# First attention layer: value projections of units 2 and 3 moved into turns 1 and 2, and those turns put into the fixed order

## The chip, the cores and the metric

One core of one Trainium2 chip runs the whole kernel. The metric is the device time of one execution in microseconds (us). Names used below: PE is the matrix engine (TensorE), DVE the vector engine, ACT the scalar engine, POOL the GpSimd engine, SP the engine that here only issues DMAs. PEld is the loading of weights into PE.

## The reference

A batch of two images, 512 channels of 64 x 64 pixels in float32, passes four residual layers. The change lies in the first, a local attention with 8 heads of 64 channels, of which this is the core:

```python
q = l2norm(gn(x) @ W_q + b_q);  q_scaled = (q + query_embedding) * softplus(temperature)
k, v = gn(x) @ W_kv + b_kv;     k = l2norm(k)             # per head
local = q_scaled . k over the 3 x 3 neighbours            # 9 scores per pixel and head
pool  = q_scaled . l2norm(k_pool)                         # 256 pooled tokens
a = softmax([local, pool])
lt = q . learnable_tokens + bias + a[:9]
out = sum over 9 neighbours lt * v + a[9:] @ v_pool
x = x + out @ W_proj + b_proj
```

The pooled tokens come from a projection with GELU, a mean over 4 x 4 pixels and a layer norm. The other three layers (deformable attention, a mixture of max pools, a linear attention) are not touched.

## The kernel before

**Layout.** Channels lie on the 128 partitions, in four chunks (cc, 0 to 3), two heads to a chunk. A unit is 1024 pixels (16 image rows) of one chunk: UN = 4 units to a chunk, 16 units in all, numbered 0 to 15. The class `Local` computes the layer, once for each of the two images. The images of keys (`kx`) and values (`vx`) of one chunk are kept with a border of zeros, so that the nine neighbours are nine shifted views.

**Turns.** `run` (L2020) goes through turns i = -4 to 16. In turn i different units are at different stages, and each stage is a Python generator that issues the instructions of one step and yields; `in_turn` takes one step of each stage after the other, ten steps to a turn. The stages of turn i:

- `norms` (L2359): for the keys and queries projected in the turn before, sums of squares on PE (L2369), a transpose on DVE (L2372), some thirteen small DVE instructions for the inverse roots (L2375 to L2382), a transpose back (L2384).
- `tap_products` and `tap_sums` for unit i+1: the query times nine shifted key images on DVE (L2447), summed over a head's channels on PE (L2474, four column tiles of 32), exponential on ACT (L2482).
- `attend` for unit i: scores against the pooled keys (L2499), exponentials on ACT (L2503), pooled values (L2509), the halves of the sums on POOL (L2518), sums of the softmax on PE (L2525, L2528), reciprocal on DVE (L2553 to L2561); then the weights go to rows in DRAM (L2566) and come back spread over the 64 channels of a head, one tap at a time (L2584).
- `weigh` for unit i-1: each tap's weights are copied to PSUM by ACT (L2600), multiplied on DVE with the output (L2605, tap 0) or with the shifted values (L2608), and added on POOL (L2613). It reads the values of its own unit and one row of the units beside it.
- `projections` (L2323): keys of unit i+4 and queries of unit i+3, and value projections (`value`, L2427: L134 on PE, L2430 on ACT), two for each unit, each 512 pixels with four matmuls (eight passes in the trace). L134 is the helper's line for all projections.
- `normed` (L2388): the roots spread over the channels on PE (L2396), multiplied on DVE (L2404); then the learned tokens (L2419).
- In turns -4 and -3 also `pooled_heads` (L2107): the keys and values of the pooled tokens. Its last part in turn -3 runs from PE (L2165, L2167: values; L2172: transposes) over DVE (L2174), POOL (power -1/2, L2179), PE (L2185), ACT (L2187), PE (L2191) to DVE (pooled keys, L2193 x4), and ends with a bound (L1029 on PE, L1031, L1032, L1427 on DVE) and the zero border of `vx` (POOL, L2017 and L2018).

**What sets the order.** Outside fixed-order turns a planner places the instructions of all engines by priority and by its own costs. A turn with `self.steady` set is a fixed-order turn: PE gets its instructions in the order in which the steps issue them, and no other; the planner still places DVE, ACT, POOL and SP. In such a turn the stages also have other steps: the tap products are made in pairs (2048 instead of 1024 elements), the values lie in steps 0 and 2, keys and queries in steps 4, 6, 7 and 8, and the second half sums go to two of the square buffers. [...]PSUM has five banks for all these products (name mm).

**Values before.** Unit 0 in turn -4, units 1 and 2 in turn -3, unit 3 in turn -2, none from -1 to 2; from turn 3 on, unit i+1 in turn i. Fixed-order turns are 3 to 11:

```python
self.steady = self.UN <= i + 1 and i < units - 4
...
values = ([ahead] if i >= self.UN - 1 and ahead is not None
          else {-4: [0], -3: [1, 2], -2: [3]}.get(i, []))
```

After the last unit of a chunk is projected, `fetch` (L2308) issues the load of the next chunk's weights (L2312) into the same buffer.

Of the kernel before, what the change touches and what calls it, by code (L numbers as in the profile page):

```python
# [50 lines left out]
def in_turn(*gens):  # L51


    gens = list(gens)
    while gens:
        gens = [g for g in gens if next(g, gens) is not gens]
# [1688 lines left out]
class Queries:  # L1745
# [29 lines left out]
    def run(self, Y, dst, fp, pp, ppo, ppd, load):  # L1775

        nc, ratio = self.nc, fp.tile([P, NH], F32, name="ksum_ratio")
        self.Y = Y
        nc.vector.reciprocal(ratio, self.ksum[:, 0, :])
        nc.vector.tensor_tensor(ratio, ratio, self.ksum[:, 1, :], ALU.mult)  # L1780
        in_turn(self.score(0, fp, pp), self.prepare(1, pp))
        for blk in range(NB):
            stages = [self.attend(blk, ratio, dst, fp, pp, ppo, ppd)]
            if 1 <= blk < NB - 1:
                stages.append(self.prepare(blk + 1, pp))
            if blk + 1 < NB:
                stages.append(chain([None], self.score(blk + 1, fp, pp)))
            if load and 0 <= blk - 3 < KC:
                stages.append(load(blk - 3))
            if load and 0 <= blk - 4 < KC:  # L1790
                st = fp.tile([P, NB, 6], F32, name="gn_st0")
                stages.append(self.statistics(Y, st, blk - 4, pp))
            in_turn(*stages)
        big = LIMIT * math.exp(-LIMIT)
        nc.vector.reciprocal(self.low, self.low)
        for t in (self.low, self.high):
            nc.vector.tensor_scalar(t, t, big, None, ALU.mult)
            self.net.at_most(t)
# [143 lines left out]
class Local:  # L1942
# [77 lines left out]
    def run(self):  # L2020


        self.nmean = self.net.stats[:, 0]
        xs = self.pooled_tokens()
        heads = self.pooled_heads(xs)
        units = KC * self.UN
        unit = lambda u: u if 0 <= u < units else None
        self.pending = []
        for i in "qkv":
            self.fetch(i, 0)  # L2030
        for i in range(-4, units + 1):
            k, q, ahead, u, before = (unit(i + n) for n in (4, 3, 1, 0, -1))
            self.steady = self.UN <= i + 1 and i < units - 4
            streams, ended = [], []
            stages = [self.norms(streams, ended)]
            if ahead is not None:
                stages.append(self.tap_products(ahead))
            if u is not None:
                stages.append(self.attend(u))
            if i == units:  # L2040
                stages.append(self.output(KC - 2))
            if before is not None:
                stages.append(self.weigh(before))
            if ahead is not None:
                stages.append(self.tap_sums(ahead))
            values = ([ahead] if i >= self.UN - 1 and ahead is not None
                      else {-4: [0], -3: [1, 2], -2: [3]}.get(i, []))
            stages.append(self.projections(k, q, values, streams))
            stages.append(self.normed(ended))
            if i < -2:  # L2050
                stages.append(islice(heads, 12 if i == -4 else None))
            if i == units - 3:
                stages.append(self.fetch_output())
            if units - 3 < i < units:
                stages.append(self.output(i - units + 2))
            if self.steady or i == units:
                with self.net.tc.manual_schedule(engines={mybir.EngineType.PE}):
                    in_turn(*stages)
            else:
                in_turn(*stages)  # L2060

        self.nc.sync.dma_start(self.next_w, self.d["w_q1"].rearrange("(kc p) o -> p kc o", p=P))
        in_turn(self.output(KC - 1))
# [746 lines left out]
```

## Time and profile before

| | us |
|---|---|
| median of 3 runs | 5074.23 |
| lowest, highest | 5073.88, 5079.57 |
| the profiled execution, its own time | 5069.52 |
| its span, first to last instruction | 5067.7 |

The page gives for each engine its busy time and its share of the span. The busy table gives the same for any stretch, with the granted PE clock (1.00 is full), the share of the DMA engines and GB/s. Start times of L2369, which stands near the start of each turn from -3 on, cut the first image's part of the layer into turns; the second image's lies some 2515 us later.

| turn, image 1 | from | us | PE busy | DVE busy | ACT busy | POOL busy |
|---|---|---|---|---|---|---|
| -3 | 194.0 | 36.2 | 35.2 | 7.8 | 7.5 | 3.4 |
| -2 | 230.2 | 23.2 | 22.2 | 11.2 | 8.1 | 0.0 |
| -1 | 253.4 | 32.2 | 29.6 | 16.4 | 10.8 | 0.0 |
| 0 | 285.6 | 35.7 | 35.7 | 20.2 | 14.7 | 5.0 |
| 1 | 321.3 | 40.7 | 37.7 | 32.8 | 24.7 | 26.2 |
| 2 | 362.0 | 45.3 | 41.8 | 28.9 | 24.7 | 26.1 |
| 3 | 407.3 | 45.6 | 43.0 | 33.2 | 26.4 | 26.2 |
| 4 | 452.9 | 42.5 | 41.8 | 32.0 | 25.3 | 26.2 |

PE's busy time includes matmuls that run at a halved clock. Lines of a timeline are: start, length, engine, line, operation, output and inputs, shape, count of merged instructions, and in brackets how long the engine was idle before it and what released it. A line of the waits reads: engine, what waited, what it waited for, us in total, times, longest.

### The profile page before, as it was taken

How to read it: one execution, taken by the hardware profiler on the slowest of the kernel's cores; microseconds unless marked ns; L12 is line 12 of the kernel's file. 1: busy time of each engine (PE TensorE's matmuls, PEld its weight loads, DVE VectorE, ACT ScalarE, POOL GpSimd, SP SyncE). 2: the span in 40 equal slices, each digit the busy share in tenths (PEclk: the TensorE clock that was granted, in tenths of full speed). 3: DMA queues.
4: the chain of work that ended last, by engine and by line, in shares of the span. 5: the costliest groups of instructions: out<-in, count | busy, mean ns of one | idle time of the engine just before them, and what ended most of it. 6: DMA issues, size and time to landing. Idle time of an engine off the chain costs nothing. (4 is left out here: it accounts for less than half of the span.)

```text
span 5067.7 us, 48015 instructions
## 1 busy us (share of the span) xinstructions
PE 4822.0 (95%) x17027; PEld 1989.3 (39%) x17027; DVE 3069.5 (61%) x4010; ACT 1818.0 (36%) x3479; POOL 1848.2 (36%) x1218
## 2 busy tenths in 40 slices
PE   7999999999999999999999999999999999999998
PEld 3423332554334444433344233335543344444333
DVE  4266777754679533477732677777536794334776
ACT  1245555334323233321112555552443232333221
POOL 0035666501320145454500456664013201454554
PEclk9999999999999999999999999999999999999999
DMA  3035556600000000211110355565000000000111
GB/s 152 3 82 141 149 146 176 166 19 10 1 3 14 2 1 1 71 55 46 63 65 3 96 139 150 147 178 148 19 10 1 17 1 1 1 1 24 40 45 44
DMA packets 124172, 307.72 MB, mean 61 GB/s; under 512 B 20818, under 2 KB 33618, under 8 KB 122388
## 3 DMA queue, kind: packets, MB, share of 16 engines
q1 hardware_dynamic: 123924, 304.58, 20.8%
q8 instruction: 136, 2.23, 0.2%
q14 instruction: 112, 0.92, 0.1%
HBM read 256.01 MB, written 48.50 MB: 60 GB/s over the span
## 5 line engine op out<-in xcount | busy, mean ns | idle before, releaser
L134 PE MATMUL mm<-big,w 128*128 128x512 f32 x2496 | 1179.5, 616 | 32.3 <-DVE big L2404 9.5
L134 PEld LDWEIGHTS mm<-big,w 128*128 128x128 f32 x2496 | 458.5, 193 | 716.9 <-issue 558.8
L2613 POOL TENSOR_TENSOR late<-late,big 128x1024 f32<-128x1024 f32 x194 | 459.9, 2371 | 228.8 <-DVE big L2608 199.9
L2447 DVE TENSOR_TENSOR prods<-qs,big 128x1024 f32<-128x1024 f32 (+1 forms) x216 | 335.4, 1570 | 66.4 <-PE tap L2474 56.2
L1643 POOL TENSOR_TENSOR big<-big 128x512 f32<-128x512 f32 x224 | 277.6, 1272 | 219.3 <-ACT big L1634 219.3
L2608 DVE TENSOR_TENSOR big<-big,mm 128x512 f32<-128x512 f32 x388 | 254.6, 681 | 114.7 <-ACT mm L2600 113.3
L2600 ACT COPY mm<-big 128x512 f32<-128x512 f32 x432 | 247.4, 596 | 123.7 <-DMA big<-rows 78.2
L1634 ACT ACTIVATE big<-mm,ed 128x256 f32<-128x256 f32 x512 | 193.6, 489 | 233.1 <-DVE top L1630 200.4
L2518 POOL TENSOR_TENSOR late<-late 128x512 f32<-128x512 f32 x92 | 115.4, 1275 | 439.2 <-ACT late L2503 415.3
L2613 POOL TENSOR_TENSOR late<-late,tap 128x1024 f32<-128x1024 f32 x94 | 221.9, 2361 | 106.5 <-DVE tap L2608 93.6
L1446 POOL TENSOR_TENSOR wq<-prob 128x512 f32<-128x512 f32 x48 | 70.8, 1497 | 501.9 <-ACT prob L1443 501.9
L1898 PE MATMUL mm<-k,w 128*128 128x512 f32 x512 | 238.4, 609 | 12.3 <-DVE k L1891 7.3
L1630 DVE TENSOR_REDUCE top<-mm 128x1 f32<-128x512 f32 x256 | 159.0, 683 | 148.2 <-PE mm L1561 148.2
L1608 PE MATMUL mm<-w,big 128*128 128x512 f32 x512 | 235.3, 603 | 0.0
L134 PE MATMUL mm<-big,wq 128*128 128x512 f32 x512 | 232.4, 603 | 2.7 <-ACT off_t L1223 2.7
L1195 PE MATMUL mm<-big,wo 128*128 128x512 f32 x512 | 234.7, 604 | 0.0
L1356 PE MATMUL acc<-big,diag 128*128 128x512 f32 x512 | 227.3, 601 | 4.6 <-ACT diag L1361 4.6
L973 POOL TENSOR_TENSOR group_stats<-group_stats,cst 128x1 f32<-128x1 f32 (+1 forms) x20 | 12.1, 621 | 560.3 <-DVE group_stats L972 500.1
L1888 DVE RECIPROCAL psD<-psD 128x512 f32<-128x512 f32 x64 | 215.1, 3361 | 1.9
L134 PE MATMUL mm<-big,big 128*128 128x512 f32 x464 | 201.7, 594 | 0.5 <-DVE b_sr L1011 0.5
L2474 PE MATMUL tap<-prods,cst 128*32 128x512 f32 x1152 | 193.1, 604 | 4.8 <-DVE prods L2447 4.3
L1443 ACT ACTIVATE prob<-mm 128x512 f32<-128x512 f32 x256 | 133.0, 603 | 171.4 <-PE mm L1440 171.1
(419 smaller groups left out, 8152.4 us busy)
## 6 DMA issues: line engine op xcount, KB each, us to landing
big<-rows SPq DMA_DIRECT2D x432, 256.0 KB, 4.2
tap<-rows SPq DMA_DIRECT2D x208, 256.0 KB, 4.1
yd<-late SPq DMA_DIRECT2D x32, 512.0 KB, 3.0
lost_all<-lost SPq DMA_DIRECT2D x128, 128.0 KB, 3.0
out<-big SPq DMA_DIRECT2D x64, 256.0 KB, 2.0
big<-in_W_kv SPq DMA_DIRECT2D x8, 1024.0 KB, 10.1
rows<-late SPq DMA_DIRECT2D x64, 128.0 KB, 3.3
big<-in_x SPq DMA_DIRECT2D x32, 256.0 KB, 3.8
```

The source lines that it names most:

```text
L134: self.nc.tensor.matmul(ps, w[:, kc, :], X[:, kc, blk * TB:(blk + 1) * TB], start=(kc == 0), stop=(kc == KC - 1))
L1195: nc.tensor.matmul(ps, w[:, kc, oc * P:(oc + 1) * P], att[:, kc, :], start=(kc == 0), stop=(kc == KC - 1))
L1356: nc.tensor.matmul(accs[b], dg, src[:, b * TB:(b + 1) * TB], start=(j == 0), stop=(j == 6))
L1608: nc.tensor.matmul(ps, X[:, kc, lo:lo + P], wv[:, kc, :], start=(kc == 0), stop=(kc == KC - 1))
L1634: nc.scalar.activation(f[:, t, :], pS[h][i][:, t % 2, :], AF.Exp, bias=ed[:, t, 2 * cc + h:2 * cc + h + 1])
L1643: nc.gpsimd.tensor_tensor(a, a, part, ALU.add)
L1888: nc.vector.reciprocal(psD, psD)
L1898: nc.tensor.matmul(ps, self.wo[:, kc, oc * P:(oc + 1) * P], qs[:, kc, :], start=(kc == 0), stop=(kc == KC - 1))
L2447: self.nc.vector.tensor_tensor(self.pair(u, k)[:, :n].rearrange("p k (y x) -> p k y x", x=W), bcast(qs.rearrange("p (y x) -> p y x", x=W), ...
L2600: nc.scalar.copy(ps, part)
L2608: nc.vector.tensor_tensor(part.rearrange("p (y x) -> p y x", x=W), self.vx[:, y:y + self.UY // 2, dx:dx + W], ps.rearrange("p (y x) -> p y ...
L2613: nc.gpsimd.tensor_tensor(out, out, t, ALU.add)
```

## The change

```diff
-            self.steady = self.UN <= i + 1 and i < units - 4
+            self.steady = 1 <= i < units - 4
...
-            values = ([ahead] if i >= self.UN - 1 and ahead is not None
-                      else {-4: [0], -3: [1, 2], -2: [3]}.get(i, []))
+            values = ([ahead] if i > 0 and ahead is not None else
+                      {-4: [0], -2: [1]}.get(i, []))
```

Turns 1 and 2 become fixed-order turns. The value projections of unit 2 move from turn -3 to turn 1, those of unit 3 from turn -2 to turn 2, and those of unit 1 from turn -3 to turn -2. The load of the next chunk's value weights follows unit 3 to turn 2. No instruction of PE is added or taken away; on DVE the nine tap products of a unit become five in the turns concerned.

In the built program PE's order in turn -3 loses three stretches of value matmuls (one matmul here is two passes in the trace):

```
 L2167 mm<-late,cst 128x512
-L134  mm<-big,w 128x512 x4
 L2165 mm<-big,late 128x512 x4
...
 L2172 mm<-cst,late 128x128 x2
-L134  mm<-big,w 128x512 x4
 L2185 mm<-cst,late 128x128 x2
...
 L2396 mm<-sq,cst 128x512 x2
-L134  mm<-big,w 128x512 x28
+L134  mm<-big,w 128x512 x20
```

DVE's order in the same turn was: the whole chain of roots, L2384, then the four L2193 and the three small instructions of the bound. It becomes:

```
L2380, L2381, L2193, L2382, L2193, L2380, L2193, L2381, L2193, L2382, L1031, L2380, L1032,
L2381, L1427, L2382, L2384
```

On POOL the two memsets of the border of `vx` now stand ahead of L2179 instead of behind it. In turns -2, -1 and 0 PE's order stays as it was, and from turn 1 on it is that of the fixed-order turns. All this is the same for both images.

## The prediction

> **What bounds the kernel now.** First the page's engine totals, then the busy table cut into stretches, then the timelines and the PE waits.
>
> ```profile
> PE 4822.0 (95%) x17027; PEld 1989.3 (39%) x17027; DVE 3069.5 (61%) x4010; ACT 1818.0 (36%) x3479; POOL 1848.2 (36%) x1218
> ```
>
> TensorE (PE) fills 95% of the span; only its work, its waits and its clock count. The stretches run from the first score matmul (L2499) of turn 1 to that of turn 4, then one fixed-order turn; image 1, then image 2:
>
> ```profile
> 319.37:448.20 128.83, 119.66 (x426) 37.22 (x425) 91.50 (x152) 74.73 (x132) 76.92 (x39) 0.97 0.51 137
> 448.20:490.74 42.54, 41.84 (x154) 13.16 (x153) 32.02 (x49) 25.32 (x46) 26.16 (x14) 1.00 0.54 142
> 2834.16:2968.90 134.74, 124.08 (x425) 38.68 (x424) 91.59 (x152) 74.58 (x132) 76.89 (x39) 0.94 0.50 131
> 2968.90:3011.45 42.55, 41.85 (x155) 13.17 (x154) 32.03 (x49) 25.25 (x46) 26.17 (x14) 1.00 0.54 143
> ```
>
> First figure: length; then busy times of PE, PEld, DVE, ACT, POOL; then the granted clock. A fixed-order turn takes 42.54 us, PE 98% busy. Turns 1 to 3 take 128.83 and 134.74, though turns 1 and 2 hold no value matmuls: they wait, and the clock falls to 0.97 and 0.94. What they wait for, in image 1:
>
> ```profile
> PE mm L2396 <- DVE sq L2384: 2.5, 1, 2.5
> PE mm L134 <- DVE big L2608: 1.9, 1, 1.9
> PE mm L2499 <- DVE late L2605: 1.7, 1, 1.7
> ```
>
> The first two lie in turns 1 and 2, the third at the entry to turn 3. After the second, at 380.12, eight passes of L134 take 6.57 us where 3.70 is usual. Now turn -3, where value matmuls leave, on PE:
>
> ```profile
> 192.98 1.12 PE L2167 MATMUL mm<-late,cst 1*128 1x512 f32 x2
> 194.03 1.07 PE L2369 MATMUL mm<-sq,cst 128*32 128x512 f32 x8
> 195.02 0.44 PE L2172 MATMUL mm<-cst,late 128*128 128x128 f32 x2
> 195.30 3.60 PE L134 MATMUL mm<-big,w 128*128 128x512 f32 x8
> 199.06 0.44 PE L2185 MATMUL mm<-cst,late 128*128 128x128 f32 x2 [0.17 <-POOL late L2179]
> 200.02 0.71 PE L2191 MATMUL mm<-late,cst 2*128 2x256 f32 x8 [0.52 <-ACT late L2187]
> 200.66 0.28 PE L1029 MATMUL mm<-qe_sq,cst 128*64 128x4 f32 x4
> 201.23 2.38 PE L2396 MATMUL mm<-sq,cst 2*128 2x512 f32 x4 [0.28 <-DVE kp L2193]
> 203.54 26.72 PE L134 MATMUL mm<-big,w 128*128 128x512 f32 x56
> ```
>
> The projection at 195.30 fills PE exactly while POOL makes its power (L2179) for L2185. On POOL and DVE:
>
> ```profile
> 196.10 2.90 POOL L2179 TENSOR_TENSOR late<-kp_norms,mhalf 128x16 f32<-128x16 f32 x1 [30.66 <-DVE kp_norms L2174]
> ```
>
> ```profile
> 198.77 0.20 DVE L2382 SCALAR_TENSOR_TENSOR mm<-mm,roots 128x32 f32<-128x32 f32 x1
> 199.00 0.72 DVE L2384 STREAM_TRANSPOSE sq<-mm 128x512 f32<-128x512 f32 x1
> 200.75 1.41 DVE L2193 TENSOR_TENSOR kp<-late,mm 128x256 f32<-128x256 f32 x4 [1.03 <-PE mm L2191]
> ```
>
> [...]a 4.08 us pause ending at 864.90 is followed by 3.5 us at 0.50[...] a 1.93 us pause at 380 was followed by half clock too. [...] at turn 3, L2605 waited 9.98 us and the transpose L2372 stood behind it until 411.55, its input done at 408.4. [...] Eight passes of L2474 took 1.06 us and four took 1.05, so the fixed order's pairs halve that work.
>
> **Step 1, value matmuls leave turn -3.** Units 1 and 2 go: 2 x 2 projections of eight passes. Back to back, two projections start 7.06 us apart from the next work (352.96 to 360.02), so 3.53 each: 4 x 3.53 = 14.1 us off PE per image. In turn -2, unit 1 replaces unit 3: nothing. ACT loses four copies (L2430) there, with idle around them: nothing.
>
> **Step 2, the cover of the pooled keys goes.** Call the start of the norm sums (L2369) T. L2185 is released at T+5.03 by POOL, projection or not; POOL's two memsets that now stand before L2179 (0.28 + 0.21) can run before its input is there at T+2: nothing. But in the built program DVE no longer runs L2193 after the root chain: its four stand among the roots, after the first two root products (L2380, L2381). The first waits for L2191 and starts, as now, 6.72 after T; everything behind waits too. Then come four L2193 (4 x 0.37), seven root steps (7 x 0.23), three small ones (3 x 0.19) = 3.66, then L2384 with 0.72: L2396 starts at T+11.15 instead of T+7.20. Of the 14.1 one projection (3.53) lay inside this stretch, so the stretch grows from 3.67 of uncovered chain to 11.15, that is +7.48. Net -14.1 + 7.5 = -6.6 us per image. Bounds: if the interleaving cost nothing, -10.6; if the pause draws a 17 us half-clock stretch, see rival A, -0.7.
>
> **Step 3, turns 1 and 2 in the fixed order.** They take in 14.1 us of value matmuls and lose their waits. From the built order, turn 1's PE, ACT and DVE rows are those of a fixed-order turn, so the question is the entry. A fixed-order turn leaves 16.74 us from the softmax sums (L2525 at 474.00) to the next turn's first scores (490.74), in which the weights go through two DMAs to the first tap. Turn 0 leaves 302.77 to 319.37, 16.6: the same. (Turn 2 leaves only 387.68 to 402.24, 14.6, with L2561 late on a full DVE; hence the wait for L2605 in turn 3.) The value projection (3.53) now lies between turn 1's first scores and L2369, as in turn 4; L2605, at 321.75 to 324.17 now, is then done before the second scores at 319.37 + 5.7 = 325.1. So three turns at 42.54 = 127.6: image 1 saves 128.83 - 127.6 = 1.2, image 2 saves 134.74 - 127.6 = 7.1, most of it clock. No fixed-order turn from 4 to 10 shows a halved clock, so I count none in 1 to 3. Upper bound: turn 1 entered as turn 3 is, +3 us and one half-clock window (1.7).
>
> **Step 4, DMAs and the rest.** Unit 3's end also fetches the next chunk's value weights (L2312, 256 KB, 4.3 us to landing): SP queues it now in turn -2, then in turn 2 among the tap copies (L2584), needed some 30 us later. Turn 6 does just that and lasts 42.54: nothing. Without that cover it would be 4.3. In the fixed order POOL's half sums (L2518) of the second half go to the square buffers and come one step earlier; POOL is busy 26.16 of 42.54: nothing. Pairing the tap products is DVE time, 32.02 of 42.54: nothing.
>
> **Sum.** 2 x -6.6 - 1.2 - 7.1 = -21.5. The pause of step 2 is longer than now, though half clock already follows it in both images (26.72 and 25.91 for 56 passes, 24.7 at full speed); I add one 3.4 us window at half speed, +1.7. So -20 of the profiled 5069.5 (span 5067.7), that is 5049.7; the median of the timed runs lies 4.7 higher, so 5054.5.
>
> **Rivals.** A, throttle: PE idles in most of 11 us in turn -3. At 1498 a 7.26 us pause and short ones after it led to 17 us at half clock, 8.5 lost. Against 3.4 and 1.7 lost there now, that is +11.9 for both images: -21.5 + 11.9 = -9.6, 5064.6. Against it: behind L2396 stand 17.7 us of dense projections, not more pauses. B, the interleaving is free, because L2191 comes earlier than I think: 2 x -4.0 more, 5046. Against: L2179's 2.90 us is on the way in any case. C, slower: the tap chain never catches up. If L2605 comes later than the second scores' matmul, PE's order, fixed, holds everything behind it. Turn 3 shows the price, 3.0 us, and image 2 a half-clock window with it (1.7 to 3.4). Paid in each of turns 1 to 3 of both images: 6 x (3.0 + 2.5) = 33, 33 - 21.5 = +11.5, 5086. It decides from L2605 later than 325.1; for it, L2605 of turn 3 came at 410.35, past its second scores; against it, turn 4 follows at once with 42.54, so the lag heals in one turn. That the change does nothing is out: the built order shows it.
>
> **Chances.** The forecast 0.72 (5048 to 5062), A 0.12, B 0.09, C 0.07. A measurement tells about 0.2%, 10 us, from no change: faster below 5064.1. Forecast, B and a small part of A lie there: 0.82; the rest of A 0.11; C 0.07. The range runs from B to just past A: 5045 to 5066.
>
> **What would show it.** Right: turns 1, 2 and 3 at 42.5 us each with clock 1.00; in turn -3 L2396 some 11 us after L2369, with 20 instead of 28 matmuls (40 passes, about 17.7 us) behind it; L2193 in four pieces on DVE. Wrong: a wait of L2499 for L2605 in turn 1; a turn over 44 us; half clock over more than 7 us in turn -3.

## The result, and the profile after

| | median, us | lowest, highest | ratio to before, 95% interval |
|---|---|---|---|
| before (same chip) | 5073.88 | 5068.96, 5079.57 | |
| changed kernel | 5050.26 | 5046.35, 5052.35 | 0.9951 [0.9941, 0.9961] |

The change takes 23.6 us off the median; the forecast was about 20 off. The profiled execution took 5046.35 us (span 5044.5), 23.2 less than the profiled one of before. The page's engine totals:

```profile
PE 4804.4 (95%) x17027; PEld 1980.2 (39%) x17027; DVE 3073.6 (61%) x3994; ACT 1817.5 (36%) x3479; POOL 1848.7 (37%) x1218
```

PE has the same 17027 matmuls and is 17.6 us less busy. No matmul was taken away, so they take less time: in turns 1 to 3 all run at full clock (1.00 instead of 0.97 and 0.94, below), and in the fixed order more of them overlap (L2474 there: 15.87 instead of 19.59 us of PE).

From here on the layer is read in two parts for each image: the **lead**, from the first matmul of L2158 in turn -4 to the first scores (L2499) of turn 1, and **turns 1 to 3**, from there to the first scores of turn 4. Here is the busy table of before for the two leads, then that of the change for lead, turns 1 to 3 and one fixed-order turn (turn 2) of image 1, then lead and turns 1 to 3 of image 2. Columns as in the prediction.

```profile
179.90:319.37 139.47, 134.82 (x421) 47.96 (x421) 56.29 (x111) 41.17 (x65) 8.41 (x7) 0.96 0.06 15
2694.60:2834.16 139.56, 134.91 (x423) 48.02 (x422) 56.25 (x111) 41.17 (x65) 8.40 (x7) 0.96 0.06 16
```

```profile
180.10:312.96 132.86, 122.01 (x389) 42.12 (x388) 55.50 (x109) 38.48 (x61) 8.40 (x7) 0.94 0.06 14
312.96:440.95 127.99, 125.60 (x457) 39.49 (x456) 94.09 (x146) 76.35 (x136) 77.01 (x39) 1.00 0.51 140
355.87:398.41 42.54, 41.84 (x154) 13.16 (x152) 32.12 (x49) 25.43 (x46) 26.17 (x14) 1.00 0.56 150
2686.30:2818.74 132.44, 121.58 (x389) 42.00 (x388) 55.51 (x109) 38.48 (x61) 8.40 (x7) 0.94 0.05 14
2818.74:2946.73 127.99, 125.60 (x457) 39.49 (x456) 93.98 (x146) 76.27 (x136) 76.99 (x39) 1.00 0.52 139
```

The lead is 6.6 and 7.1 us shorter. Turns 1 to 3, 128.83 and 134.74 before, take 127.99 in both images, at clock 1.00: 0.8 and 6.8 less. Together that is 21.3; the other 1.9 of the 23.2 lie in the rest of the program, which the change doesn't touch. Over the profiles taken here the rest varies from 4523 us (the change) to 4536 (the change again), mostly by half clock: an estimate from the mean clocks of these two profiles, 0.984 and 0.982 over some 5050 us, gives about 10 us for it. So a single execution can't place 2 us there. The same scatter is in every time below. The two parts above repeat far better, and the experiments are read by them. They aren't exact either: the two images of one kernel differ by up to 3.3 us in the lead, where stretches of half clock fall in one image only, so smaller differences in one lead are not read as gains.

In the lead, PE's idle time (length less busy) grew from 4.65 to 10.85 us while its busy time fell by 12.8: 14.1 of value matmuls gone, 1.3 more at half clock. Where the idle time stands, PE in turn -3, the same rows as were shown of before:

```profile
189.71 1.12 PE L2167 MATMUL mm<-late,cst 1*128 1x512 f32 x2
190.76 1.07 PE L2369 MATMUL mm<-sq,cst 128*32 128x512 f32 x8
191.75 0.44 PE L2172 MATMUL mm<-cst,late 128*128 128x128 f32 x2
195.80 0.69 PE L2185 MATMUL mm<-cst,late 128*128 128x128 f32 x2 [3.61 <-POOL late L2179]
197.00 1.24 PE L2191 MATMUL mm<-late,cst 2*128 2x256 f32 x8 [0.52 <-ACT late L2187]
198.74 0.39 PE L1029 MATMUL mm<-qe_sq,cst 128*64 128x4 f32 x4 [0.49 <-DVE kp L2193]
201.57 2.08 PE L2396 MATMUL mm<-sq,cst 2*128 2x512 f32 x4 [2.45 <-DVE sq L2384]
203.58 20.12 PE L134 MATMUL mm<-big,w 128*128 128x512 f32 x40
```

The projection that filled PE behind L2172 is gone, and PE waits 3.61 us for POOL. The durations show the clock: L2191 takes 1.24 instead of 0.71, L2396 2.08 where full speed gives 1.13, the 40 passes 20.12 instead of 17.65. And L2396 comes 10.81 us after L2369, not 7.20. DVE shows why:

```profile
193.89 0.20 DVE L2381 TENSOR_TENSOR mm<-mm,roots 128x32 f32<-128x32 f32 x1
198.26 0.42 DVE L2193 TENSOR_TENSOR kp<-late,mm 128x256 f32<-128x256 f32 x1 [4.17 <-PE mm L2191]
198.60 0.18 DVE L2382 SCALAR_TENSOR_TENSOR roots<-mm,roots 128x32 f32<-128x32 f32 x1
...
200.81 0.72 DVE L2384 STREAM_TRANSPOSE sq<-mm 128x512 f32<-128x512 f32 x1
```

DVE stands 4.17 us at the first L2193, which needs L2191, while the roots behind it (L2382 and the rest, ready since 194.1) wait in the same queue. PE's waits in turns 1 to 3 of image 1 are short, and none is L2499 for L2605:

```profile
PE mm L134 <- DVE big L2404: 1.6, 3, 0.5
PE mm L134 <- ACT late L2503: 0.5, 3, 0.2
PE mm L134 <- ACT sq L2335: 0.3, 1, 0.3
```

The overlap can be read from the busy table of one line alone, L2474 (the tap sums, 108 matmuls), first before, then in the change, both for turns 1 to 3 of image 1; here the second figure is PE, the third PEld:

```profile
319.37:448.20 128.83, 19.59 (x108) 3.15 (x108) 0.97 0.51 137
```

```profile
312.96:440.95 127.99, 15.87 (x108) 2.32 (x108) 1.00 0.51 140
```

The same 108 matmuls occupy PE for 3.7 us less, since more of them overlap (the prediction shows it: eight passes in 1.06 us, four in 1.05). L2499 (15.67 to 13.55) and L2369 (4.80 to 3.20) fall too. The three can't simply be added, because matmuls of two lines also overlapped before: the nine lines' PE times in turns 1 to 3 of image 1, each taken alone, add up to 125.5 us, where PE was busy for 119.66.

### The profile page after: what moved, and what is told of

It reads as the page before. It is cut to its first block, busy times and chain, and to the rows that moved or that the text cites. A ratio compares the mean times of both kernels' runs of the same rounds, so it can differ in the third digit from the quotient of the medians.

```text
span 5044.5 us, 48001 instructions
## 1 busy us (share of the span) xinstructions
PE 4804.4 (95%) x17027; PEld 1980.2 (39%) x17027; DVE 3073.6 (61%) x3994; ACT 1817.5 (36%) x3479; POOL 1848.7 (37%) x1218
## 5 line engine op out<-in xcount | busy, mean ns | idle before, releaser
L134 PE MATMUL mm<-big,w 128*128 128x512 f32 x2496 | 1169.7, 611 | 30.3 <-DVE big L2404 11.8
L134 PEld LDWEIGHTS mm<-big,w 128*128 128x128 f32 x2496 | 453.3, 192 | 712.7 <-issue 550.6
L2608 DVE TENSOR_TENSOR big<-big,mm 128x512 f32<-128x512 f32 x388 | 254.8, 682 | 120.0 <-ACT mm L2600 117.0
L1634 ACT ACTIVATE big<-mm,ed 128x256 f32<-128x256 f32 x512 | 194.1, 490 | 233.0 <-DVE top L1630 200.3
L134 PE MATMUL mm<-big,wq 128*128 128x512 f32 x512 | 232.4, 603 | 2.7 <-ACT off_t L1223 2.7
L134 PE MATMUL mm<-big,big 128*128 128x512 f32 x464 | 201.7, 594 | 0.5 <-DVE b_sr L1011 0.5
L1443 ACT ACTIVATE prob<-mm 128x512 f32<-128x512 f32 x256 | 133.0, 602 | 171.3 <-PE mm L1440 171.1
L1530 POOL TENSOR_TENSOR sq<-k 128x512 f32<-128x512 f32 x128 | 132.9, 1040 | 155.4 <-ACT k L1528 139.4
## 6 DMA issues: line engine op xcount, KB each, us to landing
big<-in_W_kv SPq DMA_DIRECT2D x8, 1024.0 KB, 10.7
```

The source lines that it names most:

```text
L134: self.nc.tensor.matmul(ps, w[:, kc, :], X[:, kc, blk * TB:(blk + 1) * TB], start=(kc == 0), stop=(kc == KC - 1))
L1634: nc.scalar.activation(f[:, t, :], pS[h][i][:, t % 2, :], AF.Exp, bias=ed[:, t, 2 * cc + h:2 * cc + h + 1])
L2608: nc.vector.tensor_tensor(part.rearrange("p (y x) -> p y x", x=W), self.vx[:, y:y + self.UY // 2, dx:dx + W], ps.rearrange("p (y x) -> p y ...
```

## The experiments

Two theories. **T1, the prediction's:** both halves of the change pay, the lead by its balance of projections and pause, turns 1 to 3 by the fixed order. **T2:** the fixed order alone does it, and moving the values only changes where PE is idle. Then: does the pause in turn -3, or the half clock on it, still cost something, and what would be a better place for the projections? Times are medians; every ratio is to the kernel before on the same chip.

### The fixed order alone

From the kernel before, one line; the values stay where they were.

```diff
-            self.steady = self.UN <= i + 1 and i < units - 4
+            self.steady = 1 <= i < units - 4
```

> Only the fixed order: turns 1 and 2 get it, the values stay in turns -4 to -2. Theory (the matmuls of turns 1 and 2 were spread by the planner's order, so order alone removes their waits, and the values leaving turn -3 give a second, separate gain): turn -3 stays at 36.2 and 34.5 us; turns 1 and 2 take a fixed-order turn less two value projections, 42.5 - 7.1 = 35.5 us each if nothing but PE bounds them, 37 to 38 if the chain of roots shows (3.5 us less cover ahead of L2396); turn 3 takes 42.5. That is 128.8 and 134.7 down to 114 to 119, 25 to 36 us less in all: 5038 to 5049, as good as the whole change or better. Rival (the waits are latencies that only the value matmuls can fill): turns 1 and 2 stay near 40 us, only the entry to turn 3 is mended, 5 to 10 us less: 5064 to 5069.

Measured: 5049.53, 0.995 [0.9937, 0.9964]. That is the whole gain of the change, with half of it; it lies just above the range that was expected. Lead and turns 1 to 3 of image 1, then of image 2:

```profile
182.39:321.72 139.33, 134.67 (x421) 47.96 (x420) 56.18 (x109) 41.16 (x65) 8.40 (x7) 0.96 0.06 15
321.72:442.69 120.97, 117.13 (x426) 35.95 (x425) 93.43 (x146) 73.56 (x132) 77.12 (x39) 0.97 0.53 146
2691.40:2829.22 137.82, 133.17 (x421) 47.27 (x421) 56.12 (x109) 41.16 (x65) 8.40 (x7) 0.98 0.06 16
2829.22:2948.65 119.43, 115.37 (x425) 35.58 (x425) 93.41 (x146) 73.62 (x132) 77.11 (x39) 0.99 0.54 147
```

Against the changed kernel the lead is 6.5 and 5.4 us longer and turns 1 to 3 are 7.0 and 8.6 shorter. L2474 again takes 15.87 us in turns 1 to 3, so the overlap comes with the order and not with the values. The four projections of each image (14.1 us) are worth about 6.5 in the lead, where the rest of them covered the pause, and cost about 7 to 9 in turns 1 and 2, where the rest of them goes into PE time that is otherwise lost: without them PE is idle for 1.5 and 1.7 us more there, and busy for 5.6 and 3.9 us more with the matmuls that both kernels have (117.13 and 115.37 us against 125.60 less 14.1), at clock 0.97 and 0.99 instead of 1.00. Turns 1 and 2 alone took 40.75 and 37.67 us here (image 2: 39.29 and 37.60), where 37 to 38 were expected at most, and still above the 35.5 that a fixed-order turn less 7.1 of values would give: waits of L2499 for L2608 and of L2396 for L2384 remain (some 1.2 us each in image 2), and in image 1 the clock is 0.97.

### The values alone

The changed kernel with the old condition for the fixed order.

```diff
-            self.steady = 1 <= i < units - 4
+            self.steady = self.UN <= i + 1 and i < units - 4
```

> Only the move of the values; turns 1 and 2 stay in the planner's order. Theory: the gain of 6.4 us per image before turn 1 stays; turns 1 and 2 have 7.1 us more matmuls each and can fill some 3 to 4 us of waits each, and turn 3 is still entered late: turns 1 to 3 grow by 6 to 10 us per image. In all 0 to +7 us: 5074 to 5081. Rival (filling the waits is what counts, not the order): turns 1 and 2 stay at 41 to 45 us, and the gain of turn -3 remains: 5060.

Measured: 5066.26, 0.9983 [0.9975, 0.9991], between the theory's 5074 to 5081 and the rival's 5060. The same four stretches:

```profile
180.04:312.93 132.89, 122.04 (x389) 42.16 (x389) 55.63 (x111) 38.48 (x61) 8.40 (x7) 0.94 0.06 14
312.93:446.91 133.98, 130.22 (x457) 41.67 (x456) 92.33 (x152) 77.38 (x136) 77.02 (x39) 0.99 0.50 134
2695.20:2828.27 133.07, 122.22 (x389) 42.10 (x389) 55.62 (x111) 38.49 (x61) 8.41 (x7) 0.94 0.06 14
2828.27:2962.80 134.53, 130.66 (x458) 41.91 (x457) 92.58 (x152) 77.44 (x136) 76.96 (x39) 0.99 0.50 133
```

The lead gains 6.6 and 6.5, as in the whole change. In turns 1 to 3 image 1 gives 5.2 back (133.98 against 128.83) and image 2 nothing (134.53 against 134.74): most of the 14.1 us of matmuls per image went into waits and half clock that were there (PE's idle time falls from 9.2 to 3.8 us in image 1 and from 10.7 to 3.9 in image 2). So values alone gain 8.1 in the two parts of both images, the order alone 25.1, the change 21.3: the gains don't add up, because the moved values fill the same slack in turns 1 to 3 that the order takes away. This kernel and the change run the same matmuls in turns 1 to 3, and the fixed order does them in 125.60 us of PE time instead of 130.22. For the change as a whole T2 holds: the lead does gain, as T1 says, but turns 1 to 3 pay it back.

### Unit 1 back in turn -3, under the pooled keys

The prediction blamed 7.5 us per image on the lost cover in turn -3. Here unit 1 returns there from turn -2.

```diff
-                      {-4: [0], -2: [1]}.get(i, []))
+                      {-4: [0], -3: [1]}.get(i, []))
```

> The change, with unit 1's values in turn -3 as before instead of -2. Theory: the chain of the pooled keys has its cover again and DVE has L2384 ahead of L2193, so L2396 comes 7.2 us after L2369 instead of 10.8; turn -2's own chain lasts 5.7 us with or without a projection in it. Turns -3 and -2 together save 3.7 us per image against the change, and the half clock there costs 1 to 2 us less each: 7 to 11 us below the change, 5039 to 5043. Rival (the pause costs nothing because turn -2 then waits in its place): as the change, 5048 to 5052.

Measured: 5051.08, 0.9952 [0.9939, 0.9966]; lead 133.0 and 132.8. No gain, as the rival said. The pause left turn -3 and came up in turn -2, whose root chain now had no projection beside it (PE in turn -2):

```profile
221.57 1.06 PE L2369 MATMUL mm<-sq,cst 128*32 128x512 f32 x6
222.99 1.05 PE L2369 MATMUL mm<-sq,cst 128*32 128x512 f32 x2 [0.37 <-ACT sq L2335]
228.69 2.08 PE L2396 MATMUL mm<-sq,cst 2*128 2x512 f32 x4 [4.66 <-DVE sq L2384]
```

PE waits 4.66 us there, 10.2 us at half clock begin inside this wait, and turn -2 takes 28.5 us instead of 23.3. The last norm sums also come later, after a short wait for ACT.

### The roots ahead of the pooled keys

Three empty steps ahead of L2193, so that DVE gets its four after the root chain.

```diff
         yield
+        yield
+        yield
+        yield
         for cc in range(KC):
```

> The change, with three more empty steps ahead of the pooled keys (L2193), so that the planner puts the root chain and L2396 before them. Theory: what turn -3 lost beyond the cover is DVE's order; L2396 starts some 5.8 us after L2369 instead of 10.8, L2191 comes behind two projections without a wait; 4 us per image less, and fewer us at half clock: 8 to 12 us below the change, 5038 to 5042. Rival (POOL's power sets the pause in any case): PE waits for L2185 as before and gains under 1 us per image, 5049.

Measured: 5047.82, 0.9946 [0.9933, 0.996]; lead 131.5 and 128.2, so 1.4 and 4.2 shorter than in the change. PE in turn -3 (lines are 3 higher here: L2372 is L2369, L2399 is L2396, L2194 is L2191):

```profile
192.43 1.07 PE L2372 MATMUL mm<-sq,cst 128*32 128x512 f32 x8
...
197.47 0.69 PE L2185 MATMUL mm<-cst,late 128*128 128x128 f32 x2 [3.61 <-POOL late L2179]
198.18 2.08 PE L2399 MATMUL mm<-sq,cst 2*128 2x512 f32 x4
200.18 10.20 PE L134 MATMUL mm<-big,w 128*128 128x512 f32 x16
210.32 0.71 PE L2194 MATMUL mm<-late,cst 2*128 2x256 f32 x8
```

L2396 comes 5.75 us after the norm sums instead of 10.81, right behind L2185. That the interleaving on DVE delays it by about 5 us is shown. What it saves is less, since the half clock remains (16 passes in 10.20 us, 7.1 at full speed) and the pooled keys' matmuls now stand further back with a wait of their own (0.49 us at L1029). The gain in the lead is 5.6 in sum, and the two images differ by half clock alone: 17.1 us of it in the lead of image 1, as in the change, and 10.2 in image 2. In the time the gain, 2.4 us against the change, can't be told from none; 8 to 12 were expected.

### The change again

Unchanged, as a partner for the runs below.

> The change itself, beside the next three on one chip: 5046 to 5053 us.

Measured: 5052.27, 0.9944 [0.993, 0.9958], on a chip on which the kernel before took 5078.06. The two leads and turns 1 to 3 add up to 260.5 us in each image (260.9 and 260.4 in the first profile).

### PE fed through the pause

The changed kernel with two more value projections per image, whose results nobody reads, in the pause of turn -3: 2 x 3.53 = 7.06 us of extra PE work for each image.

```diff
             nc.tensor.transpose(ps[:, t * P:(t + 1) * P], sums[:, t * P:(t + 1) * P], net.ident)
+        self.projected("v", 2)
...
         nc.scalar.copy(sums, ps[:, :NK])
+        self.projected("v", 2)
```

> The change, with two projections of values added in turn -3 whose results nobody reads (28 us of PE work more in all would be 14.1 if nothing hid them; the output is the reference's). They stand between L2172 and L2185 and ahead of L2191, and the planner puts L2384 back before L2193, so L2396 comes about 10 us after L2369, as in the change within 1 us, but PE is fed. Theory (the pause costs half clock behind it): no half clock over 7 us in turn -3, 1.5 to 3 us less per image although PE does more: 5044 to 5047. Rival (half clock falls on the pause itself and costs little): as the change or 1 us less, 5048 to 5051. If the two projections were not hidden: 5058.

Measured: 5048.48, 0.9943 [0.9929, 0.9956]; lead 132.1 in both images. The 7.06 us per image of extra matmuls cost nothing: the lead is even 0.3 to 0.8 shorter than in the change. PE in turn -3 (L2398 is L2396; L2371, its norm sums, stands at 190.37):

```profile
200.42 1.67 PE L2398 MATMUL mm<-sq,cst 2*128 2x512 f32 x4 [0.28 <-DVE kp L2195]
202.01 18.87 PE L134 MATMUL mm<-big,w 128*128 128x512 f32 x40
```

Half clock in turn -3 fell from 13.65 to 3.4 us, and turn -3 became 2.4 and 2.0 us shorter (30.4 and 30.5 us from norm sums to norm sums, 32.9 and 32.5 in the change). But a new stretch of 3.4 us came behind a later, shorter wait, in turn -2 of image 1 (1.13 us) and in turn -1 of image 2, and made that turn 1.7 us longer. So the lead hardly gained, and the 1.5 to 3 us that were expected didn't come: half clock behind the pause does cost some 2 us, and feeding PE there moved most of that cost to a later turn.

### One unit under each root chain

If a pause swallows projections at no cost, one unit should stay in turn -3 and one in turn -2, both with a chain to cover, and turn 1 should have none.

```diff
-            values = ([ahead] if i > 0 and ahead is not None else
-                      {-4: [0], -2: [1]}.get(i, []))
+            values = ([ahead] if i > 1 and ahead is not None else
+                      {-4: [0], -3: [1], -2: [2]}.get(i, []))
```

> The change, with one unit's values per turn before turn 0 (unit 0 in turn -4, 1 in -3, 2 in -2), none in turn 1, unit 3 in turn 2. Theory (each wait for a chain of roots takes one projection as cover for nothing, any further one is full price, and what is uncovered costs half clock besides): L2396 in turn -3 comes 7.2 us after L2369, in turn -2 5.7 us with its cover; turn 1 lasts 39 us, turn 2 42.5. Against the run with the fixed order alone two projections (7.1 us) leave turn -3 and turn 2 gains 1.3: 5.8 us per image less, 5038; against the change some 10 to 12 us less, 5038 to 5041. Rival (where the values stand does not matter, since PE does the same work): as the change, 5047 to 5052.

Measured: 5043.1, 0.9933 [0.9919, 0.9946]; on another chip once more (with the expectation below) 5042.53, 0.9929 [0.9916, 0.9943].

> The run with one unit's values per turn once more, beside the one with the split on the same chip: 5038 to 5046.

Lead and turns 1 to 3 of image 1, then of image 2, from the first of these two:

```profile
179.81:312.53 132.72, 127.98 (x405) 44.72 (x404) 56.14 (x109) 39.79 (x63) 8.39 (x7) 0.96 0.06 14
312.53:436.66 124.13, 121.12 (x441) 37.79 (x440) 93.63 (x146) 75.11 (x134) 77.10 (x39) 0.99 0.53 144
2682.40:2813.46 131.06, 126.31 (x406) 44.25 (x405) 56.09 (x109) 39.79 (x63) 8.40 (x7) 0.97 0.06 15
2813.46:2937.81 124.35, 121.08 (x441) 37.85 (x440) 93.55 (x146) 74.90 (x134) 77.05 (x39) 0.99 0.53 143
```

The lead is no longer than in the change (132.86 and 132.44), though it holds two more projections: PE is 6.0 us busier in image 1 and idle for 4.74 instead of 10.85. Turns 1 to 3 are 3.9 and 3.6 shorter: turn 1, without values, takes 39.04 and 39.27 where the change has 42.91. This version beats both kernels, by some 9 us the change on the same chip (5052.27 to 5043.1). In the lead and turns 1 to 3 of both images together it is 8.7 us shorter than the change on that chip, and 7.1 in the second run. Of the 7.1 us per image taken out of turn 1, half shows, as in the fixed order alone.

### The fixed order in turn 0 too

The last version with one more fixed-order turn.

```diff
-            self.steady = 1 <= i < units - 4
+            self.steady = 0 <= i < units - 4
```

> The same as the run with one unit's values per turn, and turn 0 in the fixed order as well. Theory: turn 0 makes its tap products in pairs, which saves some 1 to 1.5 us of PE, but its chain of roots stands without values in its cover, as in turn 1 of the run with the order alone (1 us of wait): within 2 us per image of that run, 5036 to 5042. Rival (the entry to the fixed order wants a turn with slack before it; turn -1 leaves the taps late): a wait of 3 us and half clock at turn 0, 5044 to 5050.

Measured: 5043.72, 0.9932 [0.9918, 0.9946]; lead 132.6 and 132.7, turns 1 to 3 123.7 and 124.0. Nothing that can be told from the version without it, and above the 5036 to 5042 expected: turn 0 was already full on PE before the change (35.7 of 35.7 us).

### Unit 2 split over turns -2 and -1

Turn -1 also has a wait at its L2396 (1.73 us). One of unit 2's two projections goes there. `self.turn` holds the number of the turn, and the projections of turns -2 and -1 are taken at step 3 only.

```diff
-                      {-4: [0], -3: [1], -2: [2]}.get(i, []))
+                      {-4: [0], -3: [1], -2: [2], -1: [2]}.get(i, []))
...
-        values = [(u, j) for u in uvs for j in range(2)]
-        made, taken = ((4, 6, 7, 8), (0, 2)) if self.steady else ((6, 7, 8, 9), (0, 3, 6, 9))
+        values = [(u, j) for u in uvs for j in range(2)
+                  if uvs != [2] or self.turn == j - 2]
+        made, taken = ((4, 6, 7, 8), (0, 2)) if self.steady else ((6, 7, 8, 9), (3,) if self.turn in (-2, -1) else (0, 3, 6, 9))
```

> The run with one unit's values per turn, with unit 2's two projections split: one under the chain of turn -2, the other among the tap sums of turn -1, ahead of its 1.73 us wait. Theory (one projection per chain of roots is free): turn -2 loses the projection that had no cover (3.5 us), turn -1 takes it in for its wait plus 1 to 2 us, and the half clock behind that wait (1.7 us) goes: 3 us per image less than the run it is made from, about 6 in all, 5036 to 5040. Rival (turn -1 is bound by DVE's tap products and roots, which the projection pushes back because the product buffers then come free later): turn -1 grows by the full 3.5 us, no gain: as that run, 5040 to 5046.

Measured: 5046.7, 0.9937 [0.9923, 0.995], above the range expected; lead 132.8 in both images, turns 1 to 3 124.1 and 124.2, the same as in the second run of the version not split (132.7; 124.2) on that chip. Turn -1 took the projection for nothing (32.2 us, 32.3 without it). But nothing was gained where it came from. Turns are cut at the norm sums here, so a projection at step 0 counts with the turn before: turn -3 lost it and became 3.4 us shorter in both images, and turn -2, with as many projections as before, became 3.6 longer (26.9 and 28.5 us, 23.3 and 25.0 in the version not split). PE in turn -2 of image 1 (L2371 is L2369, L2398 is L2396):

```profile
219.88 1.06 PE L2371 MATMUL mm<-sq,cst 128*32 128x512 f32 x6
220.87 1.13 PE L134 MATMUL mm<-big,w 128*128 128x512 f32 x2
221.93 1.05 PE L2371 MATMUL mm<-sq,cst 128*32 128x512 f32 x2
222.91 2.84 PE L134 MATMUL mm<-big,w 128*128 128x512 f32 x6
227.63 1.13 PE L2398 MATMUL mm<-sq,cst 2*128 2x512 f32 x4 [1.88 <-DVE sq L2386]
```

Without the projection ahead of them the norm sums come in two parts, L2396 comes 7.75 us after the first of them instead of 5.83, and one more stretch of half clock follows (1.7 us). It seems that this projection had covered ACT's squares, which the norm sums need: the run with unit 1 back in turn -3 waits for ACT at the same place (0.37 us). No run tests that alone.

## Why the prediction was right, point by point

**What bounds the kernel.** Right, but short of one thing. In turns 1 to 3 the prediction named waits and clock; the overlap of matmuls is a third part, 3.7 us per image in L2474 alone. It had noted that pairs halve that line and priced it only inside the 42.54 of a whole turn, which is why the total holds.

**Step 1, four projections of 3.53.** Right: PE's busy time in the lead fell by 12.8 and 13.3 (14.1 less 1.3 and 0.8 of half clock), and turns 1 to 3 took all of them in.

**Step 2, the lost cover and the interleaved roots, with the allowance.** The mechanism was right and the size nearly so. Forecast: L2396 at T+11.15; measured T+10.81. The two errors inside it have opposite signs: the first L2193 came at T+7.50 instead of 6.72, since the half clock stretched L2185 and L2191, and from there to L2384 took 2.55 us instead of 3.66, since L2193 and the small root steps overlap on DVE (starts 0.33 and 0.10 apart in turn, lengths 0.41 and 0.19). Forecast for the lead: -6.6 per image, +1.7 in sum for one more half-clock window, so -11.5; measured -6.6 and -7.1, -13.7. The stretch grew by 7.14 us in both images where 7.48 was worked out. The allowance is the term that was mis-sized: from L2396 on, half clock took 0.2 us more than before in image 1 and 1.4 more in image 2, but the kernel before also had a stretch of half clock in turn -2 of image 2 (24.9 us, 23.2 in image 1 with the same instructions), and the change has none there. These 1.6 us are luck in where half clock fell, and not an effect that the prediction foresaw.

**Half clock over 7 us in turn -3,** named as a sign of being wrong, did come: 13.65 us in both images, begun inside the pause, 4.6 and 3.8 us after the norm sums. Image 1, then image 2 (length, PE busy, clock):

```profile
195.38:209.03 13.65, 9.77 (x25) 0.50 0.01 2
2700.76:2714.41 13.65, 8.89 (x24) 0.50 0.00 0
```

It cost less than the 8.5 us of rival A: it is shorter than A's 17 us, and PE stood idle for 3.9 and 4.8 us of it. On L2396 and the projections behind it took about 3.4 and 3.0 us, where 3.4 and 1.7 were lost before, and on the short matmuls ahead of L2396 another 0.9. With the pause fed and 3.4 us of half clock left, turn -3 was only 2.4 and 2.0 us shorter. The sign was badly chosen: it counted time at half clock, and what counts is work done in it.

**Pauses and half clock.** The two pauses that the prediction gives, 4.08 and 1.93 us long, are each followed by half clock that began inside the pause and lasted 6.83 us (863.80 to 870.63 and 379.11 to 385.94). In turn -1 of the change 3.41 us of it came behind a wait of 1.73 us, after 3.41 us in which PE was busy for 1.68 (the projection behind it takes 5.40 instead of 3.70 us).

**Step 3, three turns in the fixed order.** Right within 0.4 us: 42.91, 42.54 and 42.54 in both images against 3 x 42.54. The 0.37 at the entry includes a wait of 0.3 for L2335 that the other turns don't have. Rival C is out: L2605 doesn't hold up L2499 at all.

**Step 4, DMAs, POOL and DVE at nothing.** Consistent: the turns that received them last 42.54.

**The sum.** Forecast -20 for the profiled execution; -13.7 and -7.6 in the two parts, -21.3, and -1.9 in a part that isn't touched. The median, 5050.26, lies halfway between the forecast's 5054.5 and the 5046 of rival B (interleaving free), so the number alone doesn't tell them apart. By its own mark B is out: L2396 is 3.6 us later than before, and with the roots first it comes 5 us earlier.

**What the prediction didn't see.** It added step 2 and step 3 as if each needed its own half of the change. Nearly all of the gain comes with the order alone; on top of it, moving the values is worth nothing (5049.53 and 5050.26). The forecast of the total holds all the same, since the two parts of the path were each worked out in their final state. Why turns 1 and 2 of image 1, with the order alone, still show half clock after waits of under 1 us isn't settled; the last section has a part of it.

## What to carry to other kernels

Work that is moved out of a stage is worth its length less the pause that it covered, and costs its length less the idle time that it fills where it lands; here 14.1 us moved were worth 5.4 to 6.5 and cost 7 to 9. So look for the dependency chains that have nothing beside them, give each just the work that covers it (one unit under each of two root chains: a further 7 to 9 us), and change one half at a time before both get the credit. Where a planner places the instructions, read the order in the queue that two chains share: a multiply put ahead of ready roots held them for 4 us.

## What the hardware showed that I had not expected

In the profiles of before and of the change, half clock shows up in whole windows of 3.41 us: of the 31 and 25 stretches each but the last covers one to five of them. It can begin inside a pause: in the change at 195.38, where PE waits from 192.19 to 195.80. Within each of the two profiles all stretches start on one grid of that pitch: in the change those at 195.38 and 260.23 are 19 windows apart, and those at 195.38 and 2700.76, in the two images, 734. The length of a wait alone didn't decide whether half clock followed, and where on the grid it fell may have. The run with the roots ahead of the pooled keys shows the first within one kernel: turn -2 has the same instructions and the same wait of 1.11 us ahead of L2396 in both images, and half clock follows in image 1 alone. These are the projections (L134) in the grid window before and in the one after, image 1, then image 2 (busy times of PE and PEld, then the clock):

```profile
226.88:230.29 3.41, 1.25 (x4) 0.68 (x4) 1.00 0.00 0
230.29:233.70 3.41, 3.41 (x5) 1.35 (x4) 0.50 0.00 0
2732.26:2735.67 3.41, 1.68 (x4) 0.38 (x2) 1.00 0.00 0
2735.67:2739.08 3.41, 2.98 (x7) 1.44 (x8) 1.00 0.02 5
```

The window before holds 1.25 us of projections in image 1 and 1.68 in image 2; with L2396 counted, PE is busy for 2.30 us in both. Two other runs fit this: the wait of 1.13 us in turn -2 of image 1 left 2.34 us in its window with one unit under each chain, and no half clock came; with the pause fed it left 1.22 us, and half clock followed (eight passes in 5.40 us instead of 3.70). What in such a window decides, no run here works out.
